# A woven four-layer graph kernel: other loads and weaving at the start, another order in the recurrence, new spacing of the plan, and a held emission order

## The chip, the cores and the metric

The kernel runs on one core of one Trainium2 chip. Times are device microseconds of the whole program. Each timed run was measured in rounds beside the kernel before on the same chip. The five engines are TensorE (PE; PEld is its weight load), VectorE (DVE), ScalarE (ACT), GpSimd (POOL) and SyncE (SP), which issues most of the transfers.

## The reference

Input are 128 graphs of 64 nodes with 256 features. Each layer normalises, clips at zero, runs one graph network and adds the result.

```python
h = jnp.maximum(_layernorm(x, axis=-1), 0.0)
x = x + _L0_gnn_ref(h, adj, ...)      # attention, 4 heads
h = jnp.maximum(_layernorm(x, axis=-1), 0.0)
x = x + _L1_gnn_ref(h, adj, ...)      # attention, 1 head
h = jnp.maximum(_layernorm(x, axis=-1), 0.0)
x = x + _L2_gnn_ref(h, nodemask, adj, ...)   # relational convolution
h = jnp.maximum(_layernorm(x, axis=-1), 0.0)
x = x + _L3_gnn_ref(h, adj, ...)      # three steps of a GRU ("the recurrence")
```

Graphs are independent. The kernel takes them in 16 groups of 8 graphs (4 tiles of 128 rows).

## The kernel before

Every group goes through three layers, a short "before" (normalisation, first adjacency product) and the recurrence. The recurrences follow one another and hold most of the matmuls; the layers of later groups are woven between. The weaving is done when the program is emitted: each job is a generator with a key (a time of the plan); the job with the lowest key emits its next piece, then its key goes up. Positive yields are work and are stretched so that the job ends when the plan says; negative yields are waits and count as they are.

```python
def add(self, name, start, end, work, wait, job, *after):
    self.jobs.append([start, max(end - start - wait, work) / work, job, name, after])

def run(self):
    while self.jobs:
        job = min((j for j in self.jobs if self.done.issuperset(j[4])), key=lambda j: j[0])
        work = next(job[2], None)
        if work is None:
            self.jobs.remove(job)
            self.done.add(job[3])
        else:
            job[0] += work * job[1] if work > 0 else -work
```

A scheduler then reorders what was emitted, by its own model of the engines; emission order is its priority. The plan of before:

```python
start = 103.0
for g in range(NG):
    if g < 2:        # groups 0 and 1 in halves of two tiles, one half in "early" buffers
        t = 32.0 * g
        units = [(0, 2, [t + x for x in (0, 32, 60, 84)], 0), (2, 2, [t + x for x in (5, 37, 65, 89)], 3 - g)]
    elif g < AHEAD:  # AHEAD = 3
        units = [(0, G, [66.0, 110.0, 150.0, 185.0], 0)]
    else:
        at = 110.0 + 96.0 * (g - AHEAD)
        units = [(0, G, [at + 73.0 * i for i in range(4)], 0)]
    # ... cut: a job for each unit and layer
for g in range(NG):
    at = start + g * 93.0
    # ... cut: what it waits for; group 0 also for the weights and all jobs in early buffers
    plan.add(("before", g), at - lead, at, 3.3, 10.0, before(g), *after)
    plan.add(("recur", g), at, at + 93.0, 68.0, 0.0, later(recur, g), ...)
```

One step of the recurrence computes two chunks of 128 features. `back`, "the way back", transposes the new state (`hT`) to rows (`hnat`) on PE and copies it on DVE; `along` multiplies it by the adjacency on PE and copies the result `aT` on DVE, for the next step. The second chunk's part before the change:

```python
            h = Gate("nn", 5, 2)
            yield h.add(whh, hT, 0) + h.add(whh, hT, 1)
            hnat = work.tile([P, G, D], F32, name="hnat")
            yield back(hnew, hnat, 0, src if last else None)
            n = Gate("nn", 5, 2)
            yield n.add(w, aT, 0) + n.add(w, aT, 1)
            # ... cut
            yield z.add(whh, hT, 0) + z.add(whh, hT, 1)
            if not last:
                new = work.tile([P, K, T], F32, name="aT")
                yield along(psum, hnat, abd, new, 0)
            yield z.add(w, aT, 0) + z.add(w, aT, 1)
```

Of the kernel before, what the change touches and what calls it, by code (L numbers as in the profile page):

```python
# [9 lines left out]
F32 = mybir.dt.float32  # L10
# [10 lines left out]
G = 4  # L21
# [23 lines left out]
class Weave:  # L45
# [11 lines left out]
    def run(self):  # L57
        while self.jobs:
            job = min((j for j in self.jobs if self.done.issuperset(j[4])), key=lambda j: j[0])
            work = next(job[2], None)  # L60
            if work is None:
                self.jobs.remove(job)
# [3 lines that stand above are left out]
# [17 lines left out]
def kernel(  # L83
# [199 lines left out]
    def recurrence(work, psum, start, src, abd, store):  # L283
# [49 lines left out]
        for i in range(LAYERS):  # L333
# [7 lines left out]
            yield z.add(whh, hT, 0)  # L341
            yield r.add(w, aT, 0)
# [20 lines left out]
            yield h.add(whh, hT, 0) + h.add(whh, hT, 1)  # L363
            hnat = work.tile([P, G, D], F32, name="hnat")
            yield back(hnew, hnat, 0, src if last else None)
            n = Gate("nn", 5, 2)
            yield n.add(w, aT, 0) + n.add(w, aT, 1)
# [4 lines left out]
            if not last:  # L372
                new = work.tile([P, K, T], F32, name="aT")
                yield along(psum, hnat, abd, new, 0)
# [3 lines left out]
            if not last:  # L378
                aT = new
# [5 lines left out]
    with ExitStack() as s1:  # L385
# [35 lines left out]
        AHEAD = 3  # L421
        W = [Layer(0, work, {"wh": 2, "es": 2, "fd": 2, "gd": 2}), Layer(1, work, {}), Layer(2, work, {"u": 2})]

        nc.scalar.dma_start(w0e[:, :, :D], rows(W0))
# [21 lines left out]
        early = prep.enter_context(tc.tile_pool(name="prep", bufs=1))  # L446
        load_group(0)
        load_group(1)
        wn, gn = loaded(early, "wn", W_loop), loaded(early, "gn", Wg_loop)
        ihn, hhn = loaded(early, "ihn", w_ih), loaded(early, "hhn", w_hh)  # L450
        load_group(2)
        wrn = [loaded(early, name, weight[i]) for i, name in enumerate(("wrn0", "wrn1", "gn"))]
# [8 lines left out]
        def attention_columns(w, heads, pieces, engine):  # L461

            for i, a in enumerate(pieces):
                ab = once.tile([P, D], F32, name="ab")
                nc.scalar.dma_start(ab, over_partitions(a, D))
                wa = once.tile([P, K, D], F32, name="wa")
                engine.tensor_tensor(wa, w[:, :, :D], ab[:, None, :].to_broadcast([P, K, D]), ALU.mult)
                nc.vector.tensor_reduce(
                    w[:, :, D + i * heads : D + (i + 1) * heads],
                    wa.rearrange("p k (h f) -> p k h f", h=heads), AX.X, ALU.add,  # L470
                )

        attention_columns(w0e, H, (a_src, a_dst), nc.gpsimd)
        nc.scalar.dma_start(w1e[:, :, :D], rows(W1))
        for i, b in enumerate((b_loop, bg_loop)):
            nc.scalar.dma_start(bl[:, i * D : (i + 1) * D], over_partitions(b[0:1], D))
        with nc.allow_non_contiguous_dma(reason="biases onto partitions"):
            nc.scalar.dma_start(bi, b_ih.rearrange("(c p) -> p c", p=P))
            nc.scalar.dma_start(bh, b_hh.rearrange("(c p) -> p c", p=P))



        def blocks(name, n, pool=once):
            t = pool.tile([P, n, P], F32, name=name)
            nc.gpsimd.memset(t, 0.0)
            return t

        EB = [blocks("eb0", G * H), blocks("eb1", G)]
        OH = [blocks(f"oh{i}", G) for i in range(2)]
        ABD = [blocks(f"abd{i}", G) for i in range(2)]  # L490
# [88 lines left out]

        def later_weights(prep):  # L580
            attention_columns(w1e, 1, (a1[:D], a1[D:]), nc.vector)
            yield 0.1
# [55 lines left out]
        EBE = [blocks("eb0e", 2 * H, early), blocks("eb1e", 2, early)]  # L638

# [31 lines left out]
        plan.add("weights", 14.0, 86.0, 24.0, 0.0, later_weights(early))  # L671
        layers = (first_layer, second_layer, third_layer)
        work_of, wait_of = (9.0, 8.2, 10.4), (38.0, 35.0, 13.5)
        users, spares = {}, []
        start = 103.0
        for g in range(NG):
            if g < 2:

                t = 32.0 * g
                units = [(0, 2, [t + x for x in (0, 32, 60, 84)], 0), (2, 2, [t + x for x in (5, 37, 65, 89)], 3 - g)]  # L680
            elif g < AHEAD:
                units = [(0, G, [66.0, 110.0, 150.0, 185.0], 0)]
            else:
                at = 110.0 + 96.0 * (g - AHEAD)
                units = [(0, G, [at + 73.0 * i for i in range(4)], 0)]
            for p0, n, at, spare in units:
                for i in range(3):
                    after = [(g, p0, i - 1)] if i > 0 else []
                    if (i, i < spare) in users:
                        after.append(users[i, i < spare])  # L690
                    users[i, i < spare] = (g, p0, i)
                    if i < spare:
                        spares.append((g, p0, i))
                    plan.add((g, p0, i), at[i], at[i + 1], work_of[i] * n / G, wait_of[i] * (1.0 if n == G else 0.0),
                             layers[i](g, p0, n, i < spare), *after)
        for g in range(NG):
            at = start + g * 93.0
            after = [(g, p0, 2) for p0 in ((0, 2) if g < 2 else (0,))] + ([("recur", g - 2)] if g > 1 else [])
            if g == 0:
                after += ["weights"] + spares  # L700
            lead = 14.0 if g == 0 else 30.0
            plan.add(("before", g), at - lead, at, 3.3, 10.0, before(g), *after)
            plan.add(("recur", g), at, at + 93.0, 68.0, 0.0, later(recur, g), *([("recur", g - 1)] if g else []), ("before", g))
# [232 lines left out]
```

## Time and profile before

| | before |
|---|---|
| median of the first three runs | 1722.49 us (1721.14 to 1729.14) |
| span of the profiled run | 1725.0 us |
| PE busy | 1596.9 us, 93% |
| first matmul / first matmul of the recurrence | 23.18 / 161.6 us |
| first store of a result / 14th | 267.1 / 1567.3 us |

The prediction below shows the shares, slices and stretches, and reads them. One small loss in every group is shown here, because it became important: the intervals between the stores of successive groups are 94, 97, 104, 104, 102, 104, 98, 100, 98, 103, 100, 104 and 91 us, 100 on average, although the plan counts 93 for each.

A line of a timeline below gives the start and the duration in us, the engine, the line of the kernel, the operation, the result and its inputs, and the count; in brackets stands how long the engine had been idle before it, and what it waited for.

### The profile page before, as it was taken

The page shows a single profiled execution, that of the slowest core. Times are in us where ns is not written, and L with a number is a line of the kernel's source. Part 1 is how long each engine was busy: PE and PEld are TensorE (multiplying, and loading weights), DVE is VectorE, ACT ScalarE, POOL GpSimd, SP SyncE. Part 2 cuts the span into 40 slices and gives each one's busy share as a digit, 9 for nine tenths or more (in the row PEclk, how much of TensorE's full clock was granted, in tenths as well). Part 3 has the DMA queues.
Part 4 walks back from the last instruction along what each step waited for, and adds up shares of the span by engine and source line. Part 5 has one row for each costly group of instructions (what it writes and reads, how often), then busy time and mean ns, then how long its engine had stood idle before and what let it go on. Part 6 is the DMA issues. An engine that isn't in the chain of part 4 may idle for free.

```text
span 1725.0 us, 16160 instructions
## 1 busy us (share of the span) xinstructions
PE 1596.9 (93%) x5689; PEld 902.1 (52%) x5689; DVE 1028.4 (60%) x2401; ACT 472.8 (27%) x910; POOL 279.9 (16%) x254
## 2 busy tenths in 40 slices
PE   4877999999998998989999999999999999999997
PEld 3554555555554554545545555554555545554543
DVE  5766673856667474664647657464665657554433
ACT  2322322222322222223222332322222222222221
POOL 2110110211111011211112212021111111111110
PEclk9977999999999999999999999999999999999998
DMA  7000000000100000000000001000000000000000
GB/s 201 7 3 1 16 4 28 19 28 16 28 19 4 28 19 25 19 28 4 19 25 20 28 3 43 4 16 25 16 13 3 25 0 16 13 4 13 0 13 15
DMA packets 45510, 34.96 MB, mean 20 GB/s; under 512 B 21612, under 2 KB 43756, under 8 KB 45420
## 3 DMA queue, kind: packets, MB, share of 16 engines
q1 hardware_dynamic: 42444, 32.52, 6.7%
q10 hardware_dynamic: 2976, 1.32, 0.3%
q8 instruction: 47, 0.77, 0.2%
q14 instruction: 43, 0.35, 0.1%
HBM read 25.30 MB, written 8.52 MB: 20 GB/s over the span
## 4 chain that ended last, share of the span: by engine, by line
PE 66%; DVE 21%; POOL 5%; issue 3%; ACT 2%; DMA 2%; SPq 0%; POOLq 0%; DVEq 0%; ACTq 0%
PE rz L295 27%; PE nn L295 13%; PE mm L231 6%; PE mm L618 5%; PE mm L250 5%; PE tp L264 4%; DVE hn L158 3%; PE tp L166 3%; DVE st L149 2%; POOL rstd L154 2%; PE tp L306 2%; POOL xg L210 2%; DVE d L329 2%; DVE hT L330 1%; PE mm L630 1%
## 5 line engine op out<-in xcount | busy, mean ns | idle before, releaser
L295 PE MATMUL rz<-hT,whh 128*128 128x512 f32 x768 | 390.8, 600 | 3.9 <-ACT z L328 3.4
L295 PE MATMUL rz<-aT,wc 128*128 128x512 f32 x768 | 388.8, 597 | 3.1 <-DVE aT L268 2.9
L325 POOL TENSOR_TENSOR d<-hT,nt 128x512 f32<-128x512 f32 x96 | 125.1, 1303 | 784.1 <-ACT nt L323 784.1
L295 PEld LDWEIGHTS rz<-aT,wc 128*128 128x128 f32 x768 | 140.2, 191 | 145.4 <-issue 128.3
L295 PEld LDWEIGHTS rz<-hT,whh 128*128 128x128 f32 x768 | 138.5, 192 | 118.9 <-issue 105.5
L295 PE MATMUL nn<-aT,wc 128*128 128x512 f32 x384 | 191.1, 597 | 0.0
L295 PE MATMUL nn<-hT,whh 128*128 128x512 f32 x384 | 190.8, 598 | 0.0
L329 DVE SCALAR_TENSOR_TENSOR d<-z,d 128x512 f32<-128x512 f32 x96 | 74.2, 773 | 102.5 <-POOL d L325 59.1
L158 DVE TENSOR_SCALAR hn<-xg,mv,rstd 128x256 f32<-128x256 f32 x256 | 101.3, 441 | 46.6 <-POOL rstd L154 46.4
L264 PEld LDWEIGHTS tp<-abd,hnat 128*128 128x128 f32 x768 | 102.0, 194 | 43.3 <-issue 31.5
L618 PE MATMUL mm<-wl,hT 128*128 128x512 f32 x248 | 122.1, 617 | 0.3 <-ACT hT L167 0.3
L166 PE MATMUL tp<-ident,hn 128*128 128x128 f32 x512 | 75.5, 285 | 50.3 <-DVE hn L158 35.7
L167 ACT ACTIVATE hT<-tp 128x512 f32<-128x512 f32 (+1 forms) x130 | 69.4, 572 | 190.0 <-PE tp L166 189.8
L149 DVE BATCH_NORM_STATS2 st<-xg 128x6 f32<-128x256 f32 x256 | 98.3, 408 | 30.5 <-POOL xg L210 25.8
L250 PEld LDWEIGHTS mm<-wh,eb 128*128 128x128 f32 x600 | 87.5, 203 | 53.7 <-issue 27.8
L250 PE MATMUL mm<-wh,eb 128*128 128x65 f32 (+1 forms) x600 | 101.8, 305 | 14.5 <-DVE eb L569 13.9
L323 ACT ACTIVATE nt<-t,bi 128x512 f32<-128x512 f32 x96 | 69.2, 720 | 166.7 <-DVE t L321 141.6
L154 POOL TENSOR_TENSOR rstd<-var,mhalf 128x4 f32<-128x4 f32 (+1 forms) x70 | 68.3, 976 | 284.2 <-DVE var L153 277.8
L320 DVE SCALAR_TENSOR_TENSOR t<-r,t 128x512 f32<-128x512 f32 x96 | 67.7, 705 | 73.5 <-ACT r L317 58.7
L264 PE MATMUL tp<-abd,hnat 128*128 128x128 f32 x768 | 103.9, 278 | 3.9 <-DVE hnat L308 2.4
L317 ACT ACTIVATE r<-rz,brz 128x512 f32<-128x512 f32 x96 | 65.8, 686 | 150.4 <-PE rz L295 150.3
L166 PEld LDWEIGHTS tp<-ident,hn 128*128 128x128 f32 x512 | 61.8, 146 | 83.7 <-issue 33.1
(161 smaller groups left out, 1842.6 us busy)
## 6 DMA issues: line engine op xcount, KB each, us to landing
out_dram<-hnat SPq DMA_DIRECT2D x16, 512.0 KB
xg<-in_x_dram SPq DMA_DIRECT2D x15, 512.0 KB
hT<-row SPq DMA_DIRECT2D x26, 256.0 KB
at<-in_adj_dram SPq DMA_DIRECT2D x64, 32.0 KB
ag<-in_adj_dram SPq DMA_DIRECT2D x16, 128.0 KB
t<-row SPq DMA_DIRECT2D x26, 64.0 KB
ihn<-in_L_gnn_w_ih_dram SPq DMA_DIRECT2D x1, 768.0 KB
hhn<-in_L_gnn_w_hh_dram SPq DMA_DIRECT2D x1, 768.0 KB
```

Source lines behind the costliest of these rows:

```text
L149: nc.vector.bn_stats(st[:, p, :], src[:, p, :])
L154: nc.gpsimd.tensor_tensor(rstd, var, mhalf[:, :n], ALU.pow)
L158: nc.vector.tensor_scalar(hn[:, p, :], src[:, p, :], mv[:, p, 0:1], rstd[:, p : p + 1], op0=ALU.subtract, op1=ALU.mult,)
L166: nc.tensor.transpose(pt[:, p * P : (p + 1) * P], hn[:, p, k * P : (k + 1) * P], ident)
L167: nc.scalar.activation(hT[:, k, :], pt[:, : n * P], AF.Relu)
L231: nc.tensor.matmul(pm[:, : D + 2 * heads], hT[:, k, p * P : (p + 1) * P], we[:, k, :], start=(k == 0), stop=(k == K - 1),)
L250: nc.tensor.matmul(pv[:, h, :], lhsT(p, h), wv[:, p, h, :], start=True, stop=True)
L264: nc.tensor.matmul(pa[:, p * P : (p + 1) * P], hnat[:, p, c * P : (c + 1) * P], abd[:, p, :], start=True, stop=True,)
L295: nc.tensor.matmul(self.pg, w[:, k, self.chunk * P : (self.chunk + 1) * P], m[:, k, :], start=(self.done == 0), stop=(self.done == self.n ...
L325: nc.gpsimd.tensor_tensor(d, hT[:, c, :], nt, ALU.subtract)
L329: nc.vector.scalar_tensor_tensor(d, z, 1.0, d, op0=ALU.add, op1=ALU.mult)
L618: nc.tensor.matmul(pm, hT[:, k, p * P : (p + 1) * P], wl[:, k, :], start=(k == 0), stop=(k == K - 1))
```

## The change

The intent is to start the recurrence sooner: only group 0 is halved, group 1 and 2 come later, the first loads come in the order of need, the columns of the attention weights are made on DVE at once, and the emission order is kept until the recurrence. In the recurrence the way back of chunk 0 moves behind two more matmuls. The diff, cut to its core:

```diff
-    def run(self):
+    def run(self, until=float("inf")):
         while self.jobs:
             job = min((j for j in self.jobs if self.done.issuperset(j[4])), key=lambda j: j[0])
+            if job[0] >= until:
+                return
@@ recurrence
             yield z.add(whh, hT, 0)
+            if i > 0:
+                aT = work.tile([P, K, T], F32, name="aT")
+                yield along(psum, hnat, abd, aT, 0)
             yield r.add(w, aT, 0)
@@
             yield h.add(whh, hT, 0) + h.add(whh, hT, 1)
+            n = Gate("nn", 5, 2)
+            yield n.add(w, aT, 0) + n.add(w, aT, 1)
             hnat = work.tile([P, G, D], F32, name="hnat")
             yield back(hnew, hnat, 0, src if last else None)
-            n = Gate("nn", 5, 2)
-            yield n.add(w, aT, 0) + n.add(w, aT, 1)
@@
-            if not last:
-                new = work.tile([P, K, T], F32, name="aT")
-                yield along(psum, hnat, abd, new, 0)
@@ loads and columns (cut: order of the other loads, memsets as a job)
-        AHEAD = 3
+        AHEAD = 2
+        AB = once.tile([P, 4, D], F32, name="AB")
+        for i, a in enumerate((a_src, a_dst)):
+            nc.scalar.dma_start(AB[:, i, :], over_partitions(a, D))
         nc.scalar.dma_start(w0e[:, :, :D], rows(W0))
-                ab = once.tile([P, D], F32, name="ab")
-                nc.scalar.dma_start(ab, over_partitions(a, D))
-                engine.tensor_tensor(wa, w[:, :, :D], ab[:, None, :].to_broadcast([P, K, D]), ALU.mult)
+                nc.vector.tensor_tensor(wa, w[:, :, :D], ab[:, None, :].to_broadcast([P, K, D]), ALU.mult)
@@ plan
-        start = 103.0
+        start, period = 93.0, 93.0
-            if g < 2:
-                t = 32.0 * g
-                units = [(0, 2, [t + x for x in (0, 32, 60, 84)], 0), (2, 2, [t + x for x in (5, 37, 65, 89)], 3 - g)]
-            elif g < AHEAD:
-                units = [(0, G, [66.0, 110.0, 150.0, 185.0], 0)]
+            if g == 0:
+                units = [(0, 2, (0.0, 30.0, 56.0, 76.0), False), (2, 2, (4.0, 34.0, 60.0, 80.0), True)]
+            elif g == 1:
+                units = [(0, G, (30.0, 76.0, 116.0, 146.0), False)]
+            elif g == 2:
+                units = [(0, G, (76.0, 130.0, 190.0, 235.0), False)]
             else:
-                at = 110.0 + 96.0 * (g - AHEAD)
-                units = [(0, G, [at + 73.0 * i for i in range(4)], 0)]
+                at = 130.0 + 93.5 * (g - 3)
+                units = [(0, G, [at + 68.0 * i for i in range(4)], False)]
@@
+        with tc.manual_schedule(engines=set(getattr(mybir.EngineType, e) for e in ('PE', 'DVE', 'Activation', 'Pool'))):
+            plan.run(until=start - 13.0)
         plan.run()
```

For groups 3 to 15 the distance between groups goes from 96 to 93.5, that between layers from 73 to 68, and the first start from 110 to 130.

More of the change, by code (lines that the diff above doesn't have):

```diff
@@ L377, in recurrence @@
             hT = hnew
-            if not last:
-                aT = new
         yield back(hT, hnat, 1, src)
@@ L448 @@
         load_group(1)
+        nc.sync.dma_start(w1e[:, :, :D], rows(W1))
+        for i, a in enumerate((a1[:D], a1[D:])):
+            nc.sync.dma_start(AB[:, 2 + i, :], over_partitions(a, D))
         wn, gn = loaded(early, "wn", W_loop), loaded(early, "gn", Wg_loop)
         ihn, hhn = loaded(early, "ihn", w_ih), loaded(early, "hhn", w_hh)
-        load_group(2)
-        wrn = [loaded(early, name, weight[i]) for i, name in enumerate(("wrn0", "wrn1", "gn"))]
+        for i, b in enumerate((b_loop, bg_loop)):
+            nc.sync.dma_start(bl[:, i * D : (i + 1) * D], over_partitions(b[0:1], D))
+        with nc.allow_non_contiguous_dma(reason="biases onto partitions"):
+            nc.sync.dma_start(bi, b_ih.rearrange("(c p) -> p c", p=P))
+            nc.sync.dma_start(bh, b_hh.rearrange("(c p) -> p c", p=P))
+        wrn = [loaded(early, name, weight[i]) for i, name in enumerate(("wrn0", "wn", "gn"))]
         make_identity(nc, ident)
@@ L459, with attention_columns @@
         nc.vector.memset(mhalf, -0.5)
-        def attention_columns(w, heads, pieces, engine):
-            for i, a in enumerate(pieces):
-                ab = once.tile([P, D], F32, name="ab")
-                nc.scalar.dma_start(ab, over_partitions(a, D))
+        def attention_columns(w, heads, pieces):
+            for i, ab in enumerate(pieces):
                 wa = once.tile([P, K, D], F32, name="wa")
-                engine.tensor_tensor(wa, w[:, :, :D], ab[:, None, :].to_broadcast([P, K, D]), ALU.mult)
+                nc.vector.tensor_tensor(wa, w[:, :, :D], ab[:, None, :].to_broadcast([P, K, D]), ALU.mult)
                 nc.vector.tensor_reduce(
@@ L471, in attention_columns @@
                 )
-        attention_columns(w0e, H, (a_src, a_dst), nc.gpsimd)
-        nc.scalar.dma_start(w1e[:, :, :D], rows(W1))
-        for i, b in enumerate((b_loop, bg_loop)):
-            nc.scalar.dma_start(bl[:, i * D : (i + 1) * D], over_partitions(b[0:1], D))
-        with nc.allow_non_contiguous_dma(reason="biases onto partitions"):
-            nc.scalar.dma_start(bi, b_ih.rearrange("(c p) -> p c", p=P))
-            nc.scalar.dma_start(bh, b_hh.rearrange("(c p) -> p c", p=P))
+        unset = []
         def blocks(name, n, pool=once):
             t = pool.tile([P, n, P], F32, name=name)
-            nc.gpsimd.memset(t, 0.0)
+            unset.append(t)
             return t
         EB = [blocks("eb0", G * H), blocks("eb1", G)]
-        OH = [blocks(f"oh{i}", G) for i in range(2)]
-        ABD = [blocks(f"abd{i}", G) for i in range(2)]
         wl = once.tile([P, K, 2 * D], F32, name="wl")
@@ L578, in attention, with clear, first_weights @@
             yield -6.0
+        def clear():
+            for t in unset:
+                nc.gpsimd.memset(t, 0.0)
+            yield 0.1
+        def first_weights():
+            attention_columns(w0e, H, (AB[:, 0, :], AB[:, 1, :]))
+            yield 0.1
+            yield -15.0
+            attention_columns(w1e, 1, (AB[:, 2, :], AB[:, 3, :]))
+            yield 0.1
         def later_weights(prep):
-            attention_columns(w1e, 1, (a1[:D], a1[D:]), nc.vector)
-            yield 0.1
             yield from relational_weights(prep, psum, wl, wn, gn, 0.5)
@@ L638 @@
         EBE = [blocks("eb0e", 2 * H, early), blocks("eb1e", 2, early)]
+        OH = [blocks(f"oh{i}", G) for i in range(2)]
+        ABD = [blocks(f"abd{i}", G) for i in range(2)]
         def first_layer(g, p0, n, spare):
@@ L670 @@
         plan = Weave()
-        plan.add("weights", 14.0, 86.0, 24.0, 0.0, later_weights(early))
+        plan.add("clear", 2.5, 3.0, 0.1, 0.0, clear())
+        plan.add("columns", 2.0, 17.0, 0.2, 15.0, first_weights())
+        plan.add("weights", 18.0, 80.0, 24.0, 0.0, later_weights(early))
         layers = (first_layer, second_layer, third_layer)
         work_of, wait_of = (9.0, 8.2, 10.4), (38.0, 35.0, 13.5)
-        users, spares = {}, []
-        start = 103.0
+        start, period = 93.0, 93.0
+        users = {}
         for g in range(NG):
-            if g < 2:
-                t = 32.0 * g
-                units = [(0, 2, [t + x for x in (0, 32, 60, 84)], 0), (2, 2, [t + x for x in (5, 37, 65, 89)], 3 - g)]
-            elif g < AHEAD:
-                units = [(0, G, [66.0, 110.0, 150.0, 185.0], 0)]
-            else:
-                at = 110.0 + 96.0 * (g - AHEAD)
-                units = [(0, G, [at + 73.0 * i for i in range(4)], 0)]
+            if g == 0:
[4 more added lines that the diff above has]
+                units = [(0, G, (76.0, 130.0, 190.0, 235.0), False)]
+            else:
+                at = 130.0 + 93.5 * (g - 3)
+                units = [(0, G, [at + 68.0 * i for i in range(4)], False)]
             for p0, n, at, spare in units:
@@ L688 @@
                     after = [(g, p0, i - 1)] if i > 0 else []
-                    if (i, i < spare) in users:
-                        after.append(users[i, i < spare])
-                    users[i, i < spare] = (g, p0, i)
-                    if i < spare:
-                        spares.append((g, p0, i))
-                    plan.add((g, p0, i), at[i], at[i + 1], work_of[i] * n / G, wait_of[i] * (1.0 if n == G else 0.0),
-                             layers[i](g, p0, n, i < spare), *after)
-        for g in range(NG):
-            at = start + g * 93.0
-            after = [(g, p0, 2) for p0 in ((0, 2) if g < 2 else (0,))] + ([("recur", g - 2)] if g > 1 else [])
-            if g == 0:
-                after += ["weights"] + spares
-            lead = 14.0 if g == 0 else 30.0
+                    if not spare:
+                        if i in users:
+                            after.append(users[i])
+                        users[i] = (g, p0, i)
+                    plan.add((g, p0, i), at[i], at[i + 1], work_of[i] * n / G, wait_of[i] * (1.0 if n == G else 0.0),
+                             layers[i](g, p0, n, spare), *after)
+            at = start + g * period
+            after = [(g, p0, 2) for p0, *_ in units] + ([("recur", g - 2)] if g > 1 else ["weights"] if g == 0 else [])
+            lead = 13.0 if g == 0 else 30.0
             plan.add(("before", g), at - lead, at, 3.3, 10.0, before(g), *after)
-            plan.add(("recur", g), at, at + 93.0, 68.0, 0.0, later(recur, g), *([("recur", g - 1)] if g else []), ("before", g))
+            plan.add(("recur", g), at, at + period, 68.0, 0.0, later(recur, g), *([("recur", g - 1)] if g else []), ("before", g))
+        with tc.manual_schedule(engines=set(getattr(mybir.EngineType, e) for e in ('PE', 'DVE', 'Activation', 'Pool'))):
+            plan.run(until=start - 13.0)
         plan.run()
```

## The prediction

> **What bounds the kernel now.** I read the page first: engine shares, then the slices.
>
> ```profile
> PE 1596.9 (93%) x5689; PEld 902.1 (52%) x5689; DVE 1028.4 (60%) x2401; ACT 472.8 (27%) x910; POOL 279.9 (16%) x254
> ...
> PE   4877999999998998989999999999999999999997
> DVE  5766673856667474664647657464665657554433
> ```
>
> TensorE (PE) is busy 93% of 1725.0 us, so nothing but its gaps can be won: 128.1 us without a matmul, plus what a slow clock costs. The first four slices (43 us each) are the only ones below 9 before the last. So I asked for busy times of stretches, split at 161.6 us, where the first recurrence matmul starts (the first start of the gate matmuls in the view of line L295).
>
> ```profile
> 0.00:161.60 161.60, 108.45 (x446) 75.17 (x447) 110.84 (x340) 48.46 (x130) 30.05 (x53) 0.86 0.20 57
> 161.60:300.00 138.40, 135.67 (x479) 76.12 (x479) 79.35 (x182) 39.13 (x78) 18.13 (x16) 1.00 0.05 15
> 300.00:1000.00 700.00, 662.25 (x2383) 372.75 (x2382) 435.30 (x1000) 192.71 (x357) 122.08 (x98) 0.99 0.07 20
> 1000.00:1640.00 640.00, 615.81 (x2166) 342.27 (x2165) 375.04 (x837) 174.43 (x320) 100.76 (x80) 0.99 0.05 13
> 1640.00:1725.00 85.00, 74.76 (x221) 35.79 (x219) 27.86 (x45) 18.02 (x27) 8.86 (x7) 0.95 0.04 14
> ```
>
> Columns: stretch, length, busy PE, PEld, DVE, ACT, POOL (instructions), granted clock, DMA share, GB/s. Before the recurrence PE idles 53.2 of 161.6 us at a mean clock of 0.86; afterwards 75.0 us in 1563 us, at 0.99. Thus 41% of all idle time lies in the first 9% of the span.
>
> The timeline says why the beginning is late:
>
> ```profile
> 12.21 0.41 ACTq L465 DMA_DIRECT2D ab<-in_L_gnn_a_dst_dram  x1
> ...
> 20.49 1.26 POOL L467 TENSOR_TENSOR wa<-w0e,ab 128x512 f32<-128x512 f32 x1 [9.40 <-DMA ab<-in_L_gnn_a_dst_dram]
> ...
> 21.96 1.53 POOL L154 TENSOR_TENSOR rstd<-var,mhalf 128x2 f32<-128x2 f32 x2
> ...
> 23.18 2.08 PE L166 MATMUL tp<-ident,hn 128*128 128x128 f32 x8 [23.18 <-DVE hn L158]
> ```
>
> The one-buffer `ab` makes the second load wait for the first product, it then queues behind the big loads, and GpSimd, waiting for it, holds back the layernorm's power, which had its input at about 9.7 us (the variances were done by then). The first matmul is at 23.18.
>
> The same timeline shows why the recurrence is late. Group 0's third layer is complete at 101.94 (its last add, L631), yet the first recurrence matmul comes 59.7 us later:
>
> ```profile
> 121.84 7.09 PE L250 MATMUL mm<-wh,eb 128*128 128x65 f32 x32 [5.63 <-DVE eb L569]
> ...
> 145.58 0.66 PE L166 MATMUL tp<-ident,hn 128*128 128x128 f32 x2 [3.63 <-DVE hn L158]
> ...
> 159.76 2.04 PE L264 MATMUL tp<-abd,hnat 128*128 128x128 f32 x16
> 161.64 1.02 PE L295 MATMUL rz<-hT,whh 128*128 128x512 f32 x2
> ```
>
> Between, PE is fed by the halves of group 1 and by group 2, all short chains through DVE. The plan makes "before" of group 0 wait for every job using the early buffers, those of group 1 too, because the recurrence's pool takes their memory.
>
> **What the Trainium skill says.** "TensorE: Matmul & The Clock Gate", Part 1, has the clock halved after an idle window of about 3.4 us, and restored after as much activity. The trace agrees in kind: after 4.96 us idle at 86.67 the eight L618 matmuls take 5.29 us, seven us later eight alike take 3.68. So gaps cost twice. The same page (Architectural detail) calls ACT and DVE queues strict FIFO, GpSimd per core; the 9.40 us wait ahead of `rstd` agrees. "DMA: Bandwidth & Descriptors", "Issuing engines are not separate DMA queues", says loads of all engines share 16 DMA engines: here the `ab` issued at 12.21 on ScalarE's queue only landed at about 20.35, amid SyncE's loads at some 200 GB/s. So order of need counts, not the queue.
>
> **Part 1, loads and columns.** Both attention vectors of each layer get their own slice of `AB` and are loaded ahead of `w0e`; the product moves to DVE; GpSimd is left the memsets after its first power. By analogy: `a_src` and `w0e`, issued by 1.3 us, were ready at 6.42, so the columns (2 products and 2 reductions of 0.69 us) occupy DVE to about 9.3, the first `hn` (2 x 0.41) and the semaphore follow: first matmul at 10.5, a gain of 12.7 us for group 0's chain. Bytes do not change.
>
> **Part 2, only group 0 halved.** I multiplied back-to-back start intervals (512 columns 0.429 us, 258 to 264 columns 0.217, 128 or 65 columns about 0.108) by the counts in the first 161.6 us: weights 21.9, normalisation transposes 7.3, value products 19.9, aggregates 13.5, layer three 12.0, the rest 8.4, together 83. So 161.6 - 83 = 78.6 us are lost ahead of the recurrence (idle, slow clock, pipeline tails).
>
> After the change the recurrence needs only the weights (21.9), group 0 (25.5) and its "before" (2.7); beside them group 1's first layer (9.6) and pieces of the next (some 7) run: 67 us. When does it start? Two ways. (a) Group 0 now ends at 101.94; 12.7 earlier is 89, and its "before" (a layernorm, 4 tiles, two adjacency products; I put 11 us from 2.4 statistics, 0.7 power, 1.6 `hn`, transposes and copies) gives 100. (b) DVE durations: a half costs 8.3, 6.7 and 6.4 us in the three layers (42.8 for both), edge bounds 2.1, "before" 7.6, columns 5.5, group 1's first layer 17.4, statistics for two more jobs 6, small ones 2: 83 us from 4.4 on, hence 87 if DVE never waited; it has some 20 us of waits at the two ends, where one chain runs alone: 107. I take 103. Lost: 103 - 67 = 36, instead of 78.6: a gain of 43.
>
> **Part 3, emission order held.** It adds no instruction. I worked out the order of emission from the plan's keys: because group 1's first layer waits for group 0's half to leave the buffer, it is emitted in one bunch with group 0's second layer, and the weights, ahead by then, pause. In order, a waiting chain cannot be passed, so I expect PE gaps of 2 to 5 us there; they are part of the 36. Holding DVE keeps group 0 in front of `edge_bounds` of later groups, which the automatic order had pulled forward (maxima of `at` at 9.2, 13.3 and 28.4 us).
>
> **Part 4, the recurrence.** Moving the way back of chunk 0 behind two `n` matmuls gives `hT` 4 x 0.43 = 1.7 us more. The chain of waits in 200 to 1640:
>
> ```profile
> PE tp L306 <- DVE hT L330: 25.8, 14, 4.8
> PE tp L166 <- DVE hnat L308: 12.2, 7, 3.2
> ...
> PE rz L295 <- DVE aT L268: 2.9, 3, 2.5
> ```
>
> In the timeline roughly half of the first row belongs to chunk 0 (2.36, 1.67, 2.50, 1.34 us, directly ahead of `nn<-aT`); the longest (4.82, 4.30) are the final way back of chunk 1, untouched. Gain up to 11. Against it, `along` of chunk 0 now stands right ahead of the matmul that reads its `aT`: copy 0.69 plus latency, about 0.9 us, in 2 of 3 layers, 32 times; the scheduler, free again here, can fill that with matmuls on `whh` or other groups. Net gain 5.
>
> **Sum.** 1725.0 - 43 - 5 = 1677 in the profile; timed runs lie about 2.5 lower (1722.49 median): 1674.5. I add 5 for the fixed order and for less work being ready when the recurrence starts: 1680.
>
> **Rivals.** First, DVE becomes the bound: it was busy 69% before 161.6 and must now do 83 us in about 100, then carry groups 1 and 2 beside the recurrence. For it: waits on DVE own most PE gaps. Against: it is at 57% in 161.6 to 300. Were it to push group 1 late, the gap would move from 120-160 to 190-210, and the time would be 1700. Second, the held order stalls PE so long that the recurrence starts at 125 and the gain shrinks to about 20: 1705. Third, the recurrence waits shift instead of vanish (`aT` for `hT`, 32 x 0.9 = 29 us unfilled): 1705. Against it, the tail, which has no filler, shows only a 0.75 us weight-load wait for `aT`. On the good side, a start at 95 and all chunk-0 waits gone: 1662.
>
> **Range and chances.** The recurrence start (95 to 120) is worth about 20 us, part 4 about 10 either way, the density of the later stretch some 5: 1660 to 1706. Two per cent is 1688; 1680 lies just under it, hence 0.66 faster, 0.31 same. Slower would need 34 us of new waits on top of no gain: 0.03.
>
> **What would show it.** First matmul near 10.5 (wrong if over 15). First recurrence matmul 95 to 112; first output store near 208, not 267. PE idle to there about 30 us, clock above 0.86. After it, PE idle about 70 us instead of 75, waits of L306 on `hT` near 15, those on `aT` under 8. I am wrong if the store interval rises above its present 97 us or a new gap opens when the second recurrence starts.

## The result

Ratios are the mean time of one kernel's fast runs over that of the other's of the same rounds, so they aren't quite the ratios of the medians quoted. The changed kernel took 1698.01 us (1695.65 to 1701.49, 4 runs) against 1723.0: ratio 0.985, 95% interval 0.982 to 0.9881. That is 1.5% faster: inside the range predicted, but less than the 2% that the prediction held to be the likelier. The way there was quite different. First the page of the changed kernel:

```profile
PE 1590.1 (94%) x5683; PEld 901.1 (53%) x5683; DVE 1013.6 (60%) x2384; ACT 470.3 (28%) x896; POOL 272.8 (16%) x245
...
PE   5567999999999999999999999999999999999997
...
PEclk9768999999999999999999999999999999999999
```

In the slices, the first four have become no better (5567 for 4877); those behind are all nines, where before several eights stood. Now the busy times of stretches, split at the first recurrence matmul, at the first store, and at the 14th. First the changed kernel, then the one before (columns as in the prediction):

```profile
0.00:157.90 157.90, 96.42 (x363) 67.14 (x364) 83.31 (x242) 40.07 (x101) 20.12 (x38) 0.79 0.21 57
157.90:266.00 108.10, 105.67 (x405) 61.84 (x404) 78.34 (x195) 31.78 (x61) 18.36 (x17) 1.00 0.06 15
266.00:1541.40 1275.40, 1241.95 (x4469) 699.46 (x4467) 792.90 (x1850) 362.05 (x679) 218.11 (x177) 1.00 0.06 18
1541.40:1697.60 156.20, 146.07 (x451) 72.69 (x449) 59.01 (x99) 36.40 (x56) 16.19 (x13) 0.98 0.03 11
```

```profile
161.60:267.10 105.50, 102.77 (x370) 57.41 (x370) 67.00 (x154) 29.38 (x55) 15.37 (x14) 1.00 0.03 8
267.10:1567.30 1300.20, 1238.92 (x4425) 696.70 (x4424) 792.35 (x1809) 358.21 (x669) 218.25 (x174) 0.99 0.06 18
1567.30:1725.00 157.70, 146.81 (x454) 72.83 (x452) 58.20 (x99) 36.70 (x56) 16.19 (x13) 0.97 0.03 11
```

The recurrence starts 3.7 us sooner, not 59. The gain is in the 13 intervals between the first and the 14th store: 1275.4 for 1300.2 us, although they hold 44 more matmuls. Thus the span falls by 27.4 = 3.7 - 2.6 + 24.8 + 1.5.

Counting PE's work as the prediction did (back-to-back intervals by counts), the first 157.9 us of the changed kernel hold 68 us of it instead of 83. They therefore lose 90 us, where before 79 were lost. The new beginning is worse by 11 us, and everything after it better by 27.4 + 11 = 38. Two questions follow: why is the start not early, and where do 38 us come from?

The waits of PE in the changed kernel up to 157.9 us (who waited for whom, us in total, times, longest) show the first; the timeline of PE shows where:

```profile
PE tp L169 <- DVE hn L161: 45.3, 8, 14.1
PE mm L253 <- DVE eb L571: 6.3, 1, 6.3
```

```profile
14.12 1.23 PE L169 MATMUL tp<-ident,hn 128*128 128x128 f32 x4 [14.12 <-DVE hn L161]
...
59.04 1.13 PE L169 MATMUL tp<-ident,hn 128*128 128x128 f32 x4 [8.27 <-DVE hn L161]
...
118.86 1.14 PE L169 MATMUL tp<-ident,hn 128*128 128x128 f32 x4 [7.45 <-DVE hn L161]
120.05 5.99 PE L630 MATMUL mm<-wl,hT 128*128 128x512 f32 x8
136.42 1.23 PE L169 MATMUL tp<-ident,hn 128*128 128x128 f32 x4 [10.38 <-DVE hn L161]
```

PE waits for layernorms (L169 is the transpose after one, L161 the normalisation on DVE). The eight L630 matmuls after a wait of 7.45 us take 5.99 us at a granted clock of 0.61; eight alike at full clock (1.00) took 3.68 in the kernel before. This is the second price of a gap, for which the prediction cites the Trainium skill, and the granted clock of 0.79 in the whole stretch says the same.

What DVE does before and during the 10.38 us (126.04 to 136.42) is the key to it. DVE's timeline of the changed kernel:

```profile
118.96 0.45 DVE L219 TENSOR_SCALAR oh<-ag 64x128 f32<-64x128 int32 x2
123.87 0.69 DVE L632 TENSOR_TENSOR u<-mm,bl 128x512 f32<-128x512 f32 x1 [4.46 <-PE mm L630]
...
127.59 0.42 DVE L152 BATCH_NORM_STATS2 st<-xg 128x6 f32<-128x256 f32 x1
...
131.56 0.39 DVE L152 BATCH_NORM_STATS2 st<-xg 128x6 f32<-128x256 f32 x1
...
134.07 0.42 DVE L152 BATCH_NORM_STATS2 st<-xg 128x6 f32<-128x256 f32 x1
...
135.95 2.03 DVE L161 TENSOR_SCALAR hn<-xg,mv,rstd 128x256 f32<-128x256 f32 x6 [1.04 <-POOL rstd L157]
```

DVE stands idle for 4.46 us in front of `u`, which needs a matmul. Behind it in the held order wait statistics whose data had been there before that wait began (L152; ten of them between 127.6 and 135), eight of them for groups 1 and 2. They run only after the second `u`, one after another, and the second half of group 0, which the recurrence needs, has its two at their end, though its data were complete at 116.2. PE waits for that half all the time.

The waits of PE from 200 us on, changed kernel, answer to those of the recurrence before:

```profile
PE tp L169 <- DVE hnat L311: 14.3, 9, 2.1
PE rz L298 <- DVE aT L271: 6.1, 9, 1.3
PE mm L253 <- DVE eb L571: 6.0, 7, 1.4
```

The row of the way back waiting for `hT` (25.8 us before) does not appear any more; `aT` rose from 2.9 to 6.1 us.

### The profile page after: what moved, and what is told of

The parts are those of the page before. It is cut to its first block, busy times and chain, and to the rows that moved or that the text cites. A ratio compares the mean times of both kernels' runs of the same rounds, so it can differ in the third digit from the quotient of the medians.

```text
span 1697.6 us, 16128 instructions
## 1 busy us (share of the span) xinstructions
PE 1590.1 (94%) x5683; PEld 901.1 (53%) x5683; DVE 1013.6 (60%) x2384; ACT 470.3 (28%) x896; POOL 272.8 (16%) x245
## 4 chain that ended last, share of the span: by engine, by line
PE 76%; DVE 14%; POOL 3%; issue 2%; ACT 2%; DMA 1%; SPq 0%; ACTq 0%; DVEq 0%; POOLq 0%
PE rz L298 33%; PE nn L298 15%; PE mm L630 6%; PE mm L234 6%; PE mm L253 5%; PE tp L267 3%; PE tp L169 3%; PE tp L309 2%; DVE hn L161 2%; DVE st L152 2%; PE mm L642 2%; DVE eb L571 1%; DVE hn L212 1%; POOL rstd L157 1%; POOL xg L213 1%
## 5 line engine op out<-in xcount | busy, mean ns | idle before, releaser
L332 DVE SCALAR_TENSOR_TENSOR d<-z,d 128x512 f32<-128x512 f32 x96 | 66.0, 688 | 119.4 <-ACT z L331 65.4
L169 PE MATMUL tp<-ident,hn 128*128 128x128 f32 x512 | 74.6, 284 | 61.4 <-DVE hn L161 45.3
L152 DVE BATCH_NORM_STATS2 st<-xg 128x6 f32<-128x256 f32 x256 | 99.2, 403 | 46.9 <-POOL xg L213 41.9
L161 DVE TENSOR_SCALAR hn<-xg,mv,rstd 128x256 f32<-128x256 f32 x256 | 101.4, 441 | 42.6 <-POOL rstd L157 42.3
L630 PE MATMUL mm<-wl,hT 128*128 128x512 f32 x248 | 119.0, 603 | 0.0
L298 PEld LDWEIGHTS nn<-aT,wc 128*128 128x128 f32 x384 | 71.5, 191 | 79.0 <-issue 75.5
L169 PEld LDWEIGHTS tp<-ident,hn 128*128 128x128 f32 x512 | 61.0, 145 | 97.5 <-issue 39.4
L322 ACT ACTIVATE t<-nn,bh 128x512 f32<-128x512 f32 x96 | 65.8, 686 | 147.1 <-PE nn L298 147.1
```

Source lines behind the costliest of these rows:

```text
L152: nc.vector.bn_stats(st[:, p, :], src[:, p, :])
L161: nc.vector.tensor_scalar(hn[:, p, :], src[:, p, :], mv[:, p, 0:1], rstd[:, p : p + 1], op0=ALU.subtract, op1=ALU.mult,)
L169: nc.tensor.transpose(pt[:, p * P : (p + 1) * P], hn[:, p, k * P : (k + 1) * P], ident)
L298: nc.tensor.matmul(self.pg, w[:, k, self.chunk * P : (self.chunk + 1) * P], m[:, k, :], start=(self.done == 0), stop=(self.done == self.n ...
L332: nc.vector.scalar_tensor_tensor(d, z, 1.0, d, op0=ALU.add, op1=ALU.mult)
L630: nc.tensor.matmul(pm, hT[:, k, p * P : (p + 1) * P], wl[:, k, :], start=(k == 0), stop=(k == K - 1))
```

## The experiments

Twelve more kernels ran, all with the right result. The table gathers them; "stores" is the time between the first and 14th store in the profiled run, "recurrence" the first matmul of it. The changed kernel was timed first, beside 1723.0 us. The experiments ran in three sets of rounds, each on another chip; the kernel before took 1725.4 us in the first (e1 to e4), 1722.4 in the second (f1, f2, f5, e4b) and 1725.1 in the third (f4, g1 to g3). So a difference of two medians of different sets is good to about 3 us only; where the ratios give another figure, it is said.

| run | edit | recurrence | stores | median us | ratio to before (95%) |
|---|---|---|---|---|---|
| before | | 161.6 | 1300 | 1723.0 | |
| changed | | 157.9 | 1275 | 1698.0 | 0.985 (0.982 to 0.9881) |
| e1_rec_only | before + new recurrence order | 160.0 | 1312 | 1737.5 | 1.0072 (1.0054 to 1.009) |
| e2_old_rec | changed, old recurrence order | 158.4 | 1286 | 1709.1 | 0.9906 (0.989 to 0.9923) |
| e3_free | changed, no hold | 125.8 | 1274 | 1666.9 | 0.9664 (0.9648 to 0.9681) |
| e4_keys | changed, mended keys | 133.5 | 1273 | 1671.0 | 0.9681 (0.9663 to 0.9699) |
| e4b_keys_free | mended keys, no hold | 109.4 | 1272 | 1650.7 | 0.9581 (0.9564 to 0.9598) |
| f4_hold_pe | changed, only PE held | 129.5 | 1274 | 1673.1 | 0.9702 (0.9685 to 0.9718) |
| f5_columns_only | before + vectors and columns | 153.8 | 1297 | 1718.8 | 0.9982 (0.9959 to 1.0005) |
| f1_free_old_spacing | e3_free, old spacing | 123.9 | 1321 | 1722.5 | 0.9997 (0.998 to 1.0015) |
| f2_rec_spacing | e1_rec_only + new spacing | 157.9 | 1263 | 1680.7 | 0.976 (0.9737 to 0.9783) |
| g1_groups_96 | e3_free, groups 96 apart | 125.7 | 1316 | 1713.1 | 0.9932 (0.9913 to 0.9951) |
| g2_layers_73 | e3_free, layers 73 apart | 124.7 | 1294 | 1686.3 | 0.9773 (0.9757 to 0.979) |
| g3_first_110 | e3_free, group 3 at 110 | 124.8 | 1339 | 1739.4 | 1.0087 (1.007 to 1.0104) |

### The order of the recurrence: e1_rec_only and e2_old_rec

The first puts the recurrence hunks of the diff into the kernel before, the second puts the old lines into the changed kernel.

```diff
 # e1_rec_only = before, with
-            yield back(hnew, hnat, 0, src if last else None)
             n = Gate("nn", 5, 2)
             yield n.add(w, aT, 0) + n.add(w, aT, 1)
+            yield back(hnew, hnat, 0, src if last else None)
 # ... and along of chunk 0 moved as in the change; e2_old_rec = the changed kernel with this undone
```

> The kernel before with the new order of the recurrence alone (way back of chunk 0 after the n matmuls, the product along of chunk 0 at the start of the next layer). Theory A: the recurrence order is what makes the stretch after the recurrence's start shorter; then the waits of the way back for hT fall from 28 us to under 6, the dense stretch shortens by 30 to 38 us and the time is 1685 to 1693 us. Rival B: the new spacing of the plan (68 instead of 73 between layers, 93.5 instead of 96 between groups, group 2 by rows) does it; then the time stays 1714 to 1722 us. The first recurrence matmul stays near 161 us under both.

> The changed kernel with the recurrence order of before. Theory A (recurrence order gives the gain, the rest costs some 10 us in the beginning): 1728 to 1738 us, slower than before, waits of the way back for hT 20 to 30 us again. Rival B (spacing of the plan gives it): 1700 to 1706 us, hT waits under 10 us.

Neither theory came out, though B was near in the second run (1709.1 us for 1700 to 1706). The new order made the kernel before 0.7% slower (1737.5 for 1725.4 us), and in the changed kernel it gives 11 us (1709.1 without it, 1698.0 with it; 10 by the ratios). The waits of PE from 200 to 1600 us in e1_rec_only:

```profile
PE tp L306 <- DVE hT L330: 22.0, 9, 5.4
PE mm L250 <- DVE eb L567: 18.6, 11, 5.4
PE rz L295 <- DVE aT L268: 10.2, 10, 2.2
```

The waits for `hT` stay at 22 us; waits for `eb`, the masked attention weights, join them with 18.6, and `aT` takes 10.2. In e2_old_rec the `hT` row was only 4.2 us although its recurrence has the old order. So the move of the way back is not what took that row away. In these two settings it worked once against the time and once for it, so it depends on what is woven in.

### The hold: e3_free and f4_hold_pe

```diff
 # e3_free
-        with tc.manual_schedule(engines=set(getattr(mybir.EngineType, e) for e in ('PE', 'DVE', 'Activation', 'Pool'))):
-            plan.run(until=start - 13.0)
+        plan.run(until=start - 13.0)
 # f4_hold_pe
-        with tc.manual_schedule(engines=set(getattr(mybir.EngineType, e) for e in ('PE', 'DVE', 'Activation', 'Pool'))):
+        with tc.manual_schedule(engines=set(getattr(mybir.EngineType, e) for e in ('PE',))):
```

> The changed kernel without the hold: the scheduler may reorder all engines from the start, nothing else. Theory C: the held order costs in the beginning, because bunched emission leaves TensorE waiting 8 to 10 us at a time; then the first recurrence matmul comes at 110 to 135 us and the time is 1670 to 1685 us. Rival D: the hold protects group 0's chain and the free order is no better: first recurrence matmul at 150 us or later, 1695 to 1710 us.

> The changed kernel with only TensorE held to the emission order, the other engines free. Theory M: it is TensorE's fixed order (weights and later groups can't fill its gaps) that costs the 31 us: 1690 to 1700 us, first recurrence matmul at 145 us or later. Rival N: it is the vector engine's fixed order, which the free scheduler changes in favour of group 0: 1666 to 1675 us, first recurrence matmul at 125 to 135 us.

Without the hold the recurrence starts 32 us sooner (125.8 for 157.9), and the whole gain reaches the end: 1666.9 us. The stretch from the first to the 14th store is the same to 2 us, so the gain lies ahead of the recurrence. What lies ahead of it in e3_free, to be set beside the first stretch of the changed kernel:

```profile
0.00:125.80 125.80, 89.17 (x362) 62.66 (x363) 77.97 (x242) 39.84 (x101) 20.55 (x38) 0.89 0.26 72
```

As many matmuls (362; 363 in the changed kernel) are done 32 us sooner, at a granted clock of 0.89 instead of 0.79. With PE alone held it takes 1673.1 us, and the recurrence starts at 129.5: PE's fixed order costs some 6 us, and, if the two add up, about 25 of the 31 come from holding DVE, ACT and POOL. Which of these three it is was not separated; the timeline above shows DVE standing in front of a wait with ready work behind it. In f4_hold_pe, where DVE was free, statistics fill the time before `u`:

```profile
97.42 0.24 DVE L153 BATCH_NORM_AGGREGATE mv<-st 128x2 f32<-128x6 f32 x2
97.58 0.72 DVE L152 BATCH_NORM_STATS2 st<-xg 128x6 f32<-128x256 f32 x2
...
99.22 0.72 DVE L152 BATCH_NORM_STATS2 st<-xg 128x6 f32<-128x256 f32 x2
...
102.32 0.69 DVE L632 TENSOR_TENSOR u<-mm,bl 128x512 f32<-128x512 f32 x1 [1.57 <-PE mm L630]
```

Here the wait ahead of `u` is 1.57 us in place of 4.46, as the statistics ran in that time.

### The keys of the plan: e4_keys and e4b_keys_free

A half's waits are not subtracted in the plan (the factor is 0 for halves). A first-layer half has 26 of planned waits and work stretched to 30, so its keys run to about 60 where the plan says 30. The next layer then starts with a key of 30 while all else is at 58, and is emitted in one piece together with group 1's first layer, which waited for the same buffers.

```diff
-                    plan.add((g, p0, i), at[i], at[i + 1], work_of[i] * n / G, wait_of[i] * (1.0 if n == G else 0.0),
+                    plan.add((g, p0, i), at[i], at[i + 1], work_of[i] * n / G, wait_of[i] if n == G else (26.0, 23.0, 13.5)[i],
```

> The changed kernel, held as it is, but the plan subtracts the waits of the halves of group 0 too (26, 23 and 13.5 instead of 0), so that their keys end where the plan says and group 1's first layer is not emitted in one bunch with group 0's second layer. Theory E: the bunching is why the recurrence still starts at 158 us; then the first recurrence matmul comes at 105 to 130 us and the time is 1668 to 1685 us. Rival F: the held order costs as much in any sequence, because the emitted latencies do not fit the chip: first recurrence matmul at 145 us or later, 1690 to 1705 us.

> The changed kernel with the keys that count the halves' waits and without the hold. Theory K: a better emission order helps the free scheduler as well: first recurrence matmul at 112 to 122 us (126 with the old keys), 1655 to 1664 us. Rival L: the scheduler undid the bunching already, the two do the same thing: 1664 to 1670 us.

With mended keys the held kernel gains 27 us (1671.0; recurrence at 133.5, a little later than expected). Without the hold as well it takes 1650.7 us, 4.2% under the kernel before. So both things cost: an emission order in lumps, and an order that can't be changed. The scheduler did not undo the lumps by itself, for the free kernel gains 14 us (by the ratios; 16 by the medians) from the keys. With mended keys the hold still costs 17 to 20 us. Stretches of e4b_keys_free:

```profile
0.00:109.40 109.40, 81.68 (x362) 58.47 (x363) 74.75 (x241) 38.71 (x101) 20.54 (x38) 0.94 0.30 82
109.40:217.10 107.70, 105.71 (x405) 61.86 (x404) 78.14 (x195) 31.84 (x62) 18.65 (x17) 1.00 0.06 16
217.10:1489.10 1272.00, 1238.86 (x4469) 697.70 (x4467) 792.39 (x1850) 362.12 (x679) 218.14 (x177) 1.00 0.06 18
```

The first 109.4 us hold as many matmuls (362) as the changed kernel's first 157.9 (363), at a granted clock of 0.94 rather than 0.79. From there on the two run alike.

### The loads and columns alone: f5_columns_only

```diff
 # before, with
+        def vectors(pieces):
+            AB = once.tile([P, 2, D], F32, name="ab")
+            for i, a in enumerate(pieces):
+                nc.scalar.dma_start(AB[:, i, :], over_partitions(a, D))
+            return AB
+        AB0 = vectors((a_src, a_dst))
         nc.scalar.dma_start(w0e[:, :, :D], rows(W0))
-        attention_columns(w0e, H, (a_src, a_dst), nc.gpsimd)
+        attention_columns(w0e, H, AB0, nc.vector)
 # ... cut: the loop over the slices; later_weights takes vectors((a1[:D], a1[D:]))
```

> The kernel before with part 1 alone in its smallest form: both vectors of a layer in their own slices, those of the first layer loaded ahead of its weights, the product on the vector engine. Theory I: the first matmul moves from 23 to about 14 us and the recurrence's start and the end move with it, 1711 to 1717 us. Rival J: the start of the recurrence is set by the halves of group 1 and by the vector engine, the gain is swallowed: first matmul at 14, time 1719 to 1724 us.

This run decides little. The first matmul came at 20.55, not 14: both powers on GpSimd were done at 13.2, but the scheduler put reductions over `at`, biases and the second layer's columns ahead of the first `hn` on DVE. The recurrence started 8 us sooner, the time fell by 3.7 us with an interval that reaches 1. What the loads in order of need are worth inside the changed kernel (first matmul at 14.12) was not measured by itself, and neither were the single halved group and the later start of groups 1 and 2.

### The spacing of groups 3 to 15: f1, f2, g1, g2, g3

```diff
 # f1_free_old_spacing: the changed kernel, no hold
-                at = 130.0 + 93.5 * (g - 3)
-                units = [(0, G, [at + 68.0 * i for i in range(4)], False)]
+                at = 110.0 + 96.0 * (g - 3)
+                units = [(0, G, [at + 73.0 * i for i in range(4)], False)]
 # f2_rec_spacing: e1_rec_only
-                at = 110.0 + 96.0 * (g - AHEAD)
-                units = [(0, G, [at + 73.0 * i for i in range(4)], 0)]
+                at = 140.0 + 93.5 * (g - AHEAD)
+                units = [(0, G, [at + 68.0 * i for i in range(4)], 0)]
 # of f1's three numbers, g1_groups_96 takes the 96 alone, g2_layers_73 the 73, g3_first_110 the 110
```

> The changed kernel without the hold, with the spacing that the plan had before for groups 3 to 15 (layers 73 apart, groups 96 apart, the first at 110). Theory G: the spacing decides how much the dense stretch gains from the recurrence order (it lost 12 us in the kernel before, and gained 11 in the changed one); then the time from the first to the fourteenth store rises from 1274 to 1295-1312 us and the time is 1688 to 1705 us. Rival H: the spacing is immaterial and the start of the plan decides; then 1664 to 1672 us.

> The kernel before with the new recurrence order and the new spacing for groups 3 to 15 (68 and 93.5, the first 37 after the recurrence's planned start as in the changed kernel). Theory G: first to fourteenth store falls from 1300 (before) and 1312 (order alone) to 1270-1282 us, the time is 1695 to 1706 us. Rival H: it stays above 1720 us.

The old spacing costs the free changed kernel 56 us (1722.5 for 1666.9), more than expected, and the new spacing wins 57 us on e1_rec_only (1680.7 for 1737.5). f1_free_old_spacing has all of the change but the hold and this spacing; its recurrence starts 38 us sooner than that of the kernel before, and yet it takes the same time (ratio 0.9997). So without the hold and without these few numbers the rest wins nothing. (By the ratios the two figures are 57 and 54 us. The held kernel with the old spacing was not run.) f2_rec_spacing has the beginning of the kernel before and neither hold nor loads nor new halves, and it beats the changed kernel by 17 us. With this spacing the waits for `hT` fall from 22 us to nothing that is listed, as in the changed kernel. The first rows of PE's waits in f2_rec_spacing, 250 to 1500 us:

```profile
PE tp L166 <- DVE hnat L308: 14.3, 9, 2.1
PE mm L250 <- DVE eb L567: 5.4, 7, 1.2
PE rz L295 <- DVE aT L268: 4.6, 8, 0.8
```

> The changed kernel without the hold, groups 96 apart instead of 93.5 (layers 68 apart, the first at 130 as in the change). Theory P: the drift against the recurrence, which advances by 93 in the plan, is what costs: 3 a group, so the lead shrinks from 38 to 2 and later groups come late; 1685 to 1715 us, the later intervals between stores worse than the early ones. Rival Q: the 73 between layers did it: then 1666 to 1675 us.

> The changed kernel without the hold, layers 73 apart instead of 68 (groups 93.5 apart, the first at 130). Theory Q (layer spacing costs): 1690 to 1715 us. Theory P (only the drift between groups costs): 1666 to 1678 us.

> The changed kernel without the hold, group 3 starting at 110 in the plan instead of 130 (so every later group 20 earlier against the recurrence; spacings 68 and 93.5 kept). Theory R: only enough lead counts: no loss, 1660 to 1672 us. Rival S: the phase of the layers against the recurrence counts, because their bursts on the vector engine then fall on other steps of the recurrence: 1680 us or more.

Each number costs by itself: 96 about 46 us, 73 about 19 (between its two theories), 110 about 72. The pure lead theory R falls, since with 110 every later group comes 20 earlier and the time is the worst of all. What is left is S, that the phase between a group's layers and the recurrence counts. Only one other start, 110, was tried, so that it is not simply too early there is not shown by g3_first_110 alone. But the three costs come to 137 us, and together, in f1_free_old_spacing, the same numbers cost only 56: a value is good or bad only beside the others.

The intervals between stores fit this too. With 96 they are 99, 97, 102, 100, 105, 102, 103, 107, 102, 102, 103, 100 and 94: they worsen as the groups drift away from the recurrence, by 2.5 each and 30 at group 15, but not steadily. In f1 the groups start 20 earlier and drift by the same 2.5, so that the 20 are made up around the middle, at group 11 for the first layers and sooner for the others, which are 73 apart. The intervals are 108, 103, 104, 98, 102, 97, 99, 100, 103, 105, 102, 103 and 96: the sixth to eighth are good, with worse ones before and after them. With 110 alone nothing is made up, and seven of the thirteen are 105 or more: 109, 105, 106, 99, 99, 102, 107, 105, 106, 110, 101, 98 and 91.

What such a collision looks like, in g3_first_110, around one wait for `hT` of 2.83 us. First its PE waits from 250 us on, then all engines in time:

```profile
PE tp L309 <- DVE hT L333: 40.8, 17, 3.6
PE mm L253 <- DVE eb L571: 15.6, 8, 5.0
```

```profile
448.79 0.67 ACT L322 ACTIVATE t<-nn,bh 128x512 f32<-128x512 f32 x1
...
450.96 0.41 DVE L161 TENSOR_SCALAR hn<-xg,mv,rstd 128x256 f32<-128x256 f32 x1 [1.19 <-POOL rstd L157]
451.29 0.69 DVE L323 SCALAR_TENSOR_TENSOR t<-r,t 128x512 f32<-128x512 f32 x1
...
456.13 0.69 DVE L333 SCALAR_TENSOR_TENSOR hT<-d,nt 128x512 f32<-128x512 f32 x1
...
456.97 0.63 PE L309 MATMUL tp<-ident,hT 128*128 128x128 f32 x4 [2.83 <-DVE hT L333]
```

The gate step L323 had its last listed input from ACT at 449.5 but stands behind a layernorm that waits 1.19 us for GpSimd's power, and starts at 451.29. Everything from there to `hT` comes later, and PE stops. Here two layernorms of other groups fell on the end of a recurrence. That collisions of this sort make up the whole difference between phases is the reading that fits the waits; only the sum was measured.

## Why the prediction was right or wrong

**Bound and loss before the recurrence: right.** PE is busy for 92 to 96% of the span in all fourteen kernels, and 79 us are lost before the recurrence in the kernel before. Runs that only moved that start moved the end by about as much: the changed kernel to e3_free 32 us of start and 31 of time, e3_free to e4b_keys_free 16 and 14 to 16. Two lines were misread. The first four slices are not the only ones below 9 before the last: three later ones show an 8. And the present store interval was 100 us on average; 97 is the second one alone.

**Part 1, first matmul at 10.5: the size was off.** It came at 14.12. The tiles of `x` arrived at 5.96 instead of 4.43, the columns began at 9.00, and two copies of the diagonal that were not in the sum, 1.56 us, and `wq` came in ahead of `hn` on DVE. The copies took 0.38 in the kernel before; here they ran beside memsets on GpSimd. The Trainium skill, "SBUF — State Buffer", "SBUF: two separate sides", describes a port pair that DVE and GpSimd lock against each other, and the traces fit it: in the three runs with memsets beside them (changed, e2_old_rec, e4_keys) the two copies took 1.46 to 2.14 us and ended 0.24 to 0.26 us after the last of these memsets, in the eleven others 0.38 us. No run was made for it.

**Part 2, the start at 103: wrong, and it is the step that failed.** The prediction added DVE's durations and some 20 us of waits for one chain and took the loss as 36 us. The runs show 157.9 and a loss of 90. The total of the durations was right (DVE was busy 83.3 us in that stretch, where 83 were summed; the terms were not compared one by one); the waits after the first 4.4 us were not 20 but some 70 us. In way (a), group 0's layers were to be complete at 89; its last add ended at 149.6, and its "before" then took 8.3 us for the 11 predicted. So the loss lies in the layers of group 0, waiting in the held order, and not in the last step.

**Part 3, gaps of 2 to 5 us: wrong in size, right in kind.** The order in lumps was seen beforehand from the keys, but its cost was put inside the 36, with 5 us more for the fixed order. The gaps are 6 to 10 us, and the hold costs 31 us. The sentence that holding DVE "keeps group 0 in front" had it the wrong way round in this order of emission: there group 0's second half stood behind statistics of groups 1 and 2. Of the rivals, the second (held order stalls, 1705) named this and was closest for the beginning, though it put the start at 125 only. Where hold and lumps are both gone, the recurrence starts at 109.4, near the 103 predicted.

**Part 4, 5 us net: the sign right by luck, the reading wrong.** In the changed kernel the new order gives 10 to 11 us, the upper figure of the prediction. In the kernel before it costs 12. The waits for `hT` that the prediction meant to remove by two matmuls went away with the spacing (f2_rec_spacing).

**Missing from the sum: the plan's spacing.** The prediction worked out no term for 96 to 93.5, 73 to 68 and 110 to 130. A denser later stretch stood only in the range, with "some 5". The spacing is worth 56 us in the free kernel. In the changed kernel as a whole, the later stretch gained 38 us where 5 were in the sum.

**The total of 1680 and the range** held because two errors, the late start (54 us worse than predicted, 90 for 36) and the denser stretch (33 better than predicted, 38 for 5), cancelled in part, and the 21 us left lay within the range. The class was missed: within 2%, which had 0.31, and not faster, which had 0.66. That the total fell so near is luck. Of the signs it named, the first matmul (14.12) stayed under its bound of 15. The start of the recurrence, the first store (266 us for 208), PE's idle time to the recurrence (61.5 us for 30) and the clock there (0.79 for over 0.86) each said plainly that the beginning had gone otherwise, and PE's idle time after it (46 us for 70) that the rest had gone better. The store interval is 98 us on average: above the 97 named, but below the 100 that it really was before.

## What to carry to other kernels

When a change touches a weaving plan, work out a term for every number in it, small ones in the steady part above all, since they are paid in every group. Test parts together and alone: an order that gains 11 us beside one spacing loses 12 beside another. And hold an order only where the emission is known to fit the chip; in a held order one wait in front of ready work holds up everything behind it, and a free order with mended keys was 47 us faster here.

## What the Trainium skill lacked or had wrong

- "TensorE: Matmul & The Clock Gate": what it states on the clock after gaps agrees in kind with the traces (5.99 us for eight matmuls after a gap, 3.68 without one); nothing was found wrong.
- The same page says that DVE and ACT are strict FIFO, but no page puts a price on a held order of several engines: 31 us of 1698, some 6 of them from PE's order.
- No page has the phase between a repeated chain and the work woven into it as a quantity to tune: 20 units of the plan, with no instruction added, moved the time from 1666.9 to 1739.4 us.
- "SBUF — State Buffer": nothing was found wrong; its locked port pair fits two copies that took 1.46 to 2.14 us beside GpSimd's memsets and 0.38 without.
